# Graph attention on one core: q at the edges for two quads beside the next pair's first layers, in two PSUM banks shared with the transposes

## The chip, the core and the metric

The kernel runs on one core of a Trainium2 chip. A core has five engines that run their own instruction streams: TensorE (PE; PEld is its weight load), VectorE (DVE), ScalarE (ACT), GpSimd (POOL) and SyncE (SP). [...] The metric is the device time of one execution in microseconds. Before the change three runs took 2072.03, 2080.5 and 2083.07 us; the median is 2080.5.

## The reference

There are 6250 nodes with 128 features and 206,250 edges, sorted by receiver. Each edge has two sets of 32 features and a cutoff. Per edge a weight vector is made by two small networks, q comes from the receiver, k and v from the sender; eight heads of 16 features give eight scores, the scores scale v, the messages are summed per receiver, and the result is added to x and normalised.

```python
w_ij = silu(edge_feats @ rad_W1 + rad_b1) @ rad_W2 + rad_b2
w_ij = w_ij + (silu(chi_scalar @ sph_W1 + sph_b1) @ sph_W2 + sph_b2)
q_i = (node_feats @ Wq).reshape(-1, 8, 16)[receivers]
k_j = (node_feats @ Wk).reshape(-1, 8, 16)[senders]
alpha = (q_i * w_ij * k_j).sum(axis=-1) / sqrt(16) * cutoffs[:, None]
v_j = (node_feats @ Wv)[senders].reshape(-1, 8, 16)
out = segment_sum(alpha[..., None] * v_j, receivers, num_segments=6250) / 16
return layernorm(x + out.reshape(-1, 128))
```

## The kernel before

**Tiles.** 128 edges are a tile, four tiles a quad (512 edges), four quads a group. There are 403 quads in 101 groups (the last has three). As the edges are sorted by receiver, the receivers of a quad lie within 32 consecutive nodes and those of a group within 128, and the kernel works with one-hot matrices relative to the first of them. (If a check of this fails at run time, a general path at the end of the kernel runs instead; with these inputs it doesn't.)

**Nodes stage.** First k and v of all nodes are computed and stored in a table in DRAM (`kv_tab`). Meanwhile VectorE makes tables of the quads' and groups' first nodes (`tables`, L257).

**Edge loop.** The loop at L519 goes over groups `g` and over four slots, which take the group's quads in the order 0, 2, 1, 3; two neighbouring slots are a pair. All engines' instruction order is the order in which the program writes them; there is no scheduler. In the slot of quad `q`, TensorE does in this order:

- `weigh` (L382): two matmuls of the activated first layers with the second layers' weights, into a bank `ph` (four such banks). ScalarE adds the bias and writes `w` (L388).
- `turn_back` (L401): four transposes of the quad before, so that edges are in partitions, into the bank `pu`.
- `take_q` (L391): q at the edges, a product of the quad's 32 q rows with a one-hot over 512 edges, into the bank `pq`.
- in slots 0 and 2 `hidden` (L364): the first layers of the next pair, four matmuls on 32 rows each into `ph` banks, and four Silu on ScalarE (L378).
- in slot 1 `sum_group` (L450), which puts the part sums of an older group in their places, and `turn_q` (L338), a transpose of the next group's x rows; in slot 3 `make_q` (L345), its product with Wq.
- `sum_quads` (L426): message sums of the group before.

Float32 matmuls are two instructions each in the profile; transposes are one.

VectorE does in a slot `scores` of the quad before (L410 multiplies the transposed bank with the gathered k, L412 sums by head, L413 scales), `multiply` (L399, u = pq times w), and `messages` (L421). One-hots (L355, L360), placements (L442, L443) and statistics (L470 on) follow in some slots.

**Gathers.** GpSimd gathers k and v of the senders by indirect DMA, one per tile (L114, four per quad), 14 quads ahead into a ring of 16 buffers. Each gather waits for a mark, an instruction of TensorE in the slot that issues it, so that gathers don't run further ahead.

**SP's queue.** All plain loads and stores of the loop go through SP in program order: in slot 0 `load_q` for the next group (four register loads and four DMAs of 32 rows of x, L163), `load_xw` (128 rows of x for the layer norm, L462), `load_rel` (four DMAs that each repeat one quad's 512 relative receivers over 32 partitions, L155); in slot 1 `load_feats` (512 KB, two groups ahead, L145). Every fourth group `statistics` (L464) also stores four tiles of out (L486).

Of the kernel before, what the change touches and what calls it, by code (L numbers as in the profile page):

```python
# [2 lines left out]

# [9 lines left out]
F32 = mybir.dt.float32  # L13
BF16 = mybir.dt.bfloat16
I32 = mybir.dt.int32
AF = mybir.ActivationFunctionType
# [7 lines left out]
P = 128  # L24
# [28 lines left out]
def gnn_kernel(ctx, tc, x, src, dst, weight, edges, rad_W1, rad_b1, rad_W2, rad_b2,  # L53
# [37 lines left out]
    rel = const.tile([P, NT], F32, name="rel")  # L91
    qb_i = const.tile([1, NG * NQ], I32, name="qb_i")
    gb_i = const.tile([1, NG], I32, name="gb_i")
    rowq = const.tile([P, NG], F32, name="rowq")
    rowp = const.tile([P, NG], F32, name="rowp")
# [35 lines left out]
    feats_of, relb_of, act_of, kv_of, hot_of, hotT_of, xq_of, q_of, msg_of = ({} for _ in range(9))  # L131
    po_of, part_of, to_of, tot_of, xw_of, y0_of, u_of = ({} for _ in range(7))

# [13 lines left out]
    def quads_in(g):  # L147
        return min(NQ, QUADS - g * NQ)

    def load_rel(g):  # L150

        relb_of[g] = gp.tile([P, EQ], BF16, name="relb")
        for j in range(NQ):
            t = g * GT + j * QT
            nc.sync.dma_start(relb_of[g][j * W:(j + 1) * W, :],  # L155
                              rel_lin[t:t + QT, :].rearrange("t e -> (t e)").partition_broadcast(W))

    def load_q(g):

        xq_of[g] = gp.tile([P, D], F32, name="xq")  # L160
        for j in range(quads_in(g)):
            r = start_of(qb_i, g * NQ + j, N - W)
            nc.sync.dma_start(xq_of[g][j * W:(j + 1) * W, :], x[ds(r, W), :])  # L163

# [17 lines left out]
    with tc.tile_pool(name="nodes", bufs=1) as nodes, \  # L182
            tc.tile_pool(name="nodes_ps", bufs=2, space=PSUM) as nps:
        chunks = [(c, min(QT, NB - c)) for c in range(0, NB, QT)]
        quads_x = order[:XQ]
        xs_of, xT_of = {}, {}
        smalls = []
# [5 lines left out]

        def load_x(k):
# [62 lines left out]
        def tables():  # L257
            nc.vector.tensor_scalar(gb, qb[:, :, 0], float(N - P), None, op0=OP.min)
            nc.vector.tensor_copy(qb_i, qb[:1].rearrange("p g j -> p (g j)"))
            nc.vector.tensor_copy(gb_i, gb[:1])  # L260
            load_q(0)
            for j in range(NQ):
                b = slice(j * W, (j + 1) * W)
                nc.vector.tensor_scalar(roww[b, :], row[b, :], float(j * W), None, op0=OP.subtract)
                nc.vector.tensor_tensor(rowq[b], qb[b, :, j], gb[b], op=OP.subtract)
            nc.vector.tensor_scalar(rowq, rowq, roww, None, op0=OP.add)
            nc.vector.tensor_copy(rowwp, roww)
            nc.vector.tensor_copy(colp, col)
# [34 lines left out]
        for k in range(8):  # L303
            load_x(k)
            if k == 5:
                nc.sync.dma_start(dst_i, dst)
# [3 lines left out]
        for i, (k, n) in enumerate(work):  # L310
# [9 lines left out]
            if k + 8 < len(chunks):  # L320
                load_x(k + 8)
            if k == 4:
# [13 lines left out]

    with tc.tile_pool(name="ps", bufs=1, space=PSUM) as pp:
        def turn_q(g):  # L338
            n = quads_in(g) * W
            pt = pp.tile([P, EQ], F32, name="ph", bufs=4)  # L340
            nc.tensor.transpose(pt[:, :n], xq_of[g][:n, :], ident[:n, :n])  # L341
            xq_of[g] = gp.tile([P, P], F32, name="xqT")
            nc.scalar.activation(xq_of[g][:, :n], pt[:, :n], AF.Copy)

        def make_q(g):  # L345

            n = quads_in(g) * W
            pt = pp.tile([P, EQ], F32, name="ph", bufs=4)
            nc.tensor.matmul(pt[:n, :D], xq_of[g][:, :n], wq, start=True, stop=True)  # L349
            q_of[g] = gp.tile([P, D], F32, name="q")  # L350
            nc.scalar.activation(q_of[g][:n, :], pt[:n, :D], AF.Copy)  # L351

        def one_hots_T(g):
# [9 lines left out]

        def hidden(pair):  # L364

            for q in pair:
                g, j = divmod(q, NQ)
                r0, c0 = 2 * R * (j // 2), EQ * (j % 2)
                for i in range(2):
                    ph = pp.tile([P, EQ], F32, name="ph", bufs=4)  # L370
                    r = slice(r0 + i * R, r0 + (i + 1) * R)
                    o = nc.tensor.matmul(ph, w1[r, :], feats_of[g][r, c0:c0 + EQ],  # L372
                                         start=True, stop=True)
                    act_of[q, i] = ph
            for q in pair:
                for i in range(2):
                    act = ep.tile([P, EQ], F32, name="act", bufs=8)
                    nc.scalar.activation(act, act_of[q, i], AF.Silu, bias=b1[:, i:i + 1])  # L378
                    act_of[q, i] = act
            return o  # L380

# [8 lines left out]

        def take_q(q):  # L391
            g, j = divmod(q, NQ)
            b = slice(j * W, (j + 1) * W)
            pq = pp.tile([P, EQ], F32, name="pq")
            return pq, nc.tensor.matmul(pq, q_of[g][b, :], hotT_of[g][b, :], start=True, stop=True)  # L395

        def multiply(q, pq, w):
            u_of[q] = ep.tile([P, EQ], F32, name="u")
            nc.vector.tensor_tensor(u_of[q], pq, w, op=OP.mult)  # L399

        def turn_back(q):  # L401

            pu = pp.tile([P, QT, D], F32, name="pu")
            for t in range(QT):
                o = nc.tensor.transpose(pu[:, t, :], u_of[q][:, t * P:(t + 1) * P], ident)  # L405
            return pu, o
# [51 lines left out]

        def load_xw(g):
            r = start_of(gb_i, g, N - P)  # L460
            xw_of[g] = gp.tile([P, D], F32, name="xw")
            nc.sync.dma_start(xw_of[g], x[ds(r, P), :])  # L462

        def statistics(g):  # L464
# [4 lines left out]
            k = g - first + 1  # L469
            nc.vector.tensor_tensor(y0[:, k - 1, :], tot_of[g], xw_of[g], op=OP.add)  # L470
            st = gp.tile([P, 6], F32, name="st")
# [31 lines left out]
        def verdict():  # L503
# [5 lines left out]
            nc.vector.tensor_scalar(general, found, 0.0, None, op0=OP.is_gt)  # L509

        turn_q(0)
        make_q(0)
# [3 lines left out]
        load_rel(1)  # L516
        hidden(pairs[0])
        before = None
        for g in range(NG):  # L519
            last = g == NG - 1  # L520
            for slot, j in enumerate((0, 2, 1, 3)):
                q = g * NQ + j
                i = g * NQ + slot
                if q >= QUADS:
                    continue
                if slot == 0 and 2 <= g:
# [12 lines left out]
                if slot == 1 and 2 <= g:  # L539
                    sum_group(g - 2)  # L540
                if slot == 1 and g + 1 < NG:
                    turn_q(g + 1)
                if slot == 3:
                    make_q(g + 1)
                if 1 <= g:
                    for t in ((), (0, 1), (2, 3))[slot] if last else ((), (0, 1), (2,), (3,))[slot]:
                        marks[3] = sum_quads(g - 1, t)
# [4 lines left out]
                multiply(q, pq, w)  # L552
                if before is not None:
                    messages(before, alpha)
                before = q
                if slot == 0:
                    if g + 1 < NG:
                        load_q(g + 1)
                    if 1 <= g:
                        load_xw(g - 1)  # L560
                        if g + 1 < NG:
                            load_rel(g + 1)
                if slot == 1:
# [4 lines left out]
                    if last:  # L568
                        place(g)
                        load_xw(g)  # L570
                if slot == 2 and g + 1 < NG:
# [178 lines left out]
```

## Time and profile before

One execution was profiled. It took 2093.36 us, with a span of 2091.3 us from its first to its last instruction.

| what | value |
|---|---|
| median of the runs | 2080.5 us |
| profiled execution / its span | 2093.36 us / 2091.3 us |
| mean granted TensorE clock | 0.967 |
| TensorE busy | 1919.3 us (92%) |
| VectorE busy | 1411.4 us (67%) |
| ScalarE busy | 1000.9 us (48%) |
| GpSimd busy | 1526.5 us (73%) |
| DMA engines busy, mean in the loop | about 0.5 |

How to read the lines: a group's line in the profile gives source line, engine, operation, what it writes and reads, shapes and count, then busy time in all and the mean of one in ns, then the engine's idle time just before such instructions with what ended it. A waits line says who waited for whom: microseconds in all, number of waits, longest. A timeline line gives start and duration in us, engine, line and operation; several instructions of one kind are merged (x4). In a line of a single source line's instructions stand shortest, median and longest duration in ns, and the first and last start. A windows line gives start and end, its length, busy time and count of PE, PEld, DVE, ACT and POOL, then the granted TensorE clock, the DMA engines' share and GB/s.

### The profile page before, as it was taken

To read this page: it belongs to the slowest core of one execution; us is meant where nothing else is said; L and a number is where in the kernel's file an instruction comes from. 1 tells how busy PE (TensorE), PEld (TensorE's weight loads), DVE (VectorE), ACT (ScalarE), POOL (GpSimd) and SP (SyncE) were. 2 spreads that over 40 slices of the span, in tenths; PEclk is the share of its full clock that TensorE was granted. 3 is DMA by queue.
4 is the path that set the end of the run, shared out by engine and by line. 5 is a ranking of instruction groups with operands and counts; after the bars stand their busy time and mean duration, and the time that the engine had idled before them with its cause. 6 is when DMAs were issued, how large, how long until landed. Compare 5 with 4: busy or idle time off the path is not lost.

```text
span 2091.3 us, 33176 instructions
## 1 busy us (share of the span) xinstructions
PE 1919.3 (92%) x9843; PEld 920.2 (44%) x9843; DVE 1411.4 (67%) x2874; ACT 1000.9 (48%) x1826; POOL 1526.5 (73%) x1620
## 2 busy tenths in 40 slices
PE   8998999989999989988998989899989999899897
PEld 7444444444444434444444444444444444444443
DVE  6676766767766766766766767667667667667666
ACT  2444545544544445444445445445445444454453
POOL 6777777777777777777777777777777777777750
PEclk9999999999999999999999999999999999999998
DMA  8545455454454454445544554554554544544540
GB/s 300 156 151 153 139 154 154 138 155 145 147 157 145 146 148 151 150 146 149 153 144 143 152 152 139 155 155 139 153 149 143 157 144 146 157 144 147 149 123 14
DMA packets 166853, 310.49 MB, mean 148 GB/s; under 512 B 46530, under 2 KB 99212, under 8 KB 166668
## 3 DMA queue, kind: packets, MB, share of 16 engines
q0 software_dynamic: 76864, 209.29, 34.3%
q1 hardware_dynamic: 88316, 98.64, 14.5%
q8 instruction: 79, 1.29, 0.2%
q14 instruction: 106, 0.87, 0.1%
q10 hardware_dynamic: 1488, 0.40, 0.1%
HBM read 294.70 MB, written 13.46 MB: 147 GB/s over the span
## 4 chain that ended last, share of the span: by engine, by line
PE 76%; ACT 9%; DMA 5%; issue 3%; SPq 3%; DVE 2%; POOL 1%; ACTq 0%; DVEq 0%
PE ph L386 32%; PE pq L395 14%; PE ph L372 11%; PE pu L405 8%; PE po L431 6%; ACT act L378 6%; DMA out<-y 2%; DMA xq<-in_x 2%; PE ph L453 2%; PE ph L349 2%; POOL msg L114 1%; SPq L163 1%; ACT y L483 1%; SPq L119 1%; PE ph L341 1%
## 5 line engine op out<-in xcount | busy, mean ns | idle before, releaser
L114 POOL DMA_INDIRECT kv<-kv_tab,src_i x1580 | 1494.8, 946 | 486.2 <-issue 261.4
L386 PE MATMUL ph<-act,w 128*128 128x512 f32 x1612 | 837.0, 644 | 78.6 <-ACT act L378 78.6
L410 DVE TENSOR_TENSOR m<-pu,kv 128x512 f32<-128x512 f32 x403 | 278.6, 691 | 557.6 <-PE pu L405 554.4
L378 ACT ACTIVATE act<-ph,b 128x512 f32<-128x512 f32 x806 | 498.5, 686 | 252.8 <-PE ph L372 239.9
L388 ACT ACTIVATE w<-ph,bsum 128x512 f32<-128x512 f32 x403 | 276.5, 686 | 456.9 <-PE ph L386 455.3
L386 PEld LDWEIGHTS ph<-act,w 128*128 128x128 f32 x1612 | 285.1, 197 | 432.4 <-issue 248.1
L395 PE MATMUL pq<-hotT,q 32*128 32x512 f32 x806 | 452.8, 641 | 0.0
L372 PE MATMUL ph<-feats,w 32*128 32x512 f32 x1612 | 398.5, 629 | 0.0
L405 PEld LDWEIGHTS pu<-ident,u 128*128 128x128 f32 x1612 | 204.1, 144 | 242.2 <-issue 155.6
L399 DVE TENSOR_TENSOR u<-pq,w 128x512 f32<-128x512 f32 x403 | 274.6, 681 | 23.7 <-ACT w L388 14.3
L412 DVE TENSOR_REDUCE side<-m 128x32 f32<-128x512 f32 x403 | 280.1, 695 | 13.7
L421 DVE TENSOR_TENSOR msg<-kv,side 128x512 f32<-128x512 f32 x403 | 272.8, 677 | 0.0
L405 PE MATMUL pu<-ident,u 128*128 128x128 f32 x1612 | 247.4, 277 | 12.7 <-DVE u L399 12.7
L372 PEld LDWEIGHTS ph<-feats,w 32*128 32x128 f32 x1612 | 158.2, 185 | 73.1 <-issue 56.1
L431 PE MATMUL po<-msg,hot 128*32 128x128 f32 x3224 | 161.4, 295 | 2.9 <-ACT part L448 2.9
L395 PEld LDWEIGHTS pq<-hotT,q 32*128 32x128 f32 x806 | 118.6, 184 | 69.7 <-issue 69.7
L431 PEld LDWEIGHTS po<-msg,hot 128*32 128x32 f32 x3224 | 75.8, 113 | 108.8 <-issue 91.3
L457 ACT ACTIVATE tot<-ph 128x128 f32<-128x128 f32 x101 | 28.0, 277 | 148.2 <-PE ph L455 139.8
L413 DVE TENSOR_TENSOR side<-side,scale 128x32 f32<-128x32 f32 x403 | 80.4, 200 | 13.8
L341 PE MATMUL ph<-ident,xq 128*128 128x128 f32 (+1 forms) x101 | 30.1, 298 | 60.8 <-DMA xq<-in_x 60.4
L351 ACT ACTIVATE q<-ph 128x128 f32<-128x128 f32 (+1 forms) x101 | 27.5, 272 | 93.1 <-PE ph L349 88.2
L360 DVE TENSOR_TENSOR hot<-rel,side 128x512 f32<-128x512 f32 x101 | 68.7, 681 | 0.0
(83 smaller groups left out, 837.2 us busy)
## 6 DMA issues: line engine op xcount, KB each, us to landing
feats<-in_edges SPq DMA_DIRECT2D x101, 512.0 KB
kv<-kv_tab,src_i POOLq DMA_INDIRECT x1580
relb<-rel_lin SPq DMA_DIRECT2D x404, 32.0 KB
xw<-in_x SPq DMA_DIRECT2D x101, 64.0 KB
out<-y SPq DMA_DIRECT2D x101, 64.0 KB
xq<-in_x SPq DMA_DIRECT2D x403, 16.0 KB
kv_tab<-kv SPq DMA_DIRECT2D x12, 512.0 KB
act<-in_x SPq DMA_DIRECT2D x12, 256.0 KB
```

The costliest lines, as they stand in the source:

```text
L114: return nc.gpsimd.indirect_dma_start(out=o, out_offset=None, in_=table, in_offset=bass.IndirectOffsetOnAxis(ap=index, axis=0))
L372: o = nc.tensor.matmul(ph, w1[r, :], feats_of[g][r, c0:c0 + EQ], start=True, stop=True)
L378: nc.scalar.activation(act, act_of[q, i], AF.Silu, bias=b1[:, i:i + 1])
L386: o = nc.tensor.matmul(pw, w2[:, i, :], act_of[q, i], start=(i == 0), stop=(i == 1))
L388: nc.scalar.activation(w, pw, AF.Identity, bias=bsum)
L395: return pq, nc.tensor.matmul(pq, q_of[g][b, :], hotT_of[g][b, :], start=True, stop=True)
L399: nc.vector.tensor_tensor(u_of[q], pq, w, op=OP.mult)
L405: o = nc.tensor.transpose(pu[:, t, :], u_of[q][:, t * P:(t + 1) * P], ident)
L410: nc.vector.tensor_tensor(m, pu, kv_of[q][:, :, :D], op=OP.mult)
L412: nc.vector.tensor_reduce(alpha, m.rearrange("p t (h e) -> p t h e", e=HD), AX.X, OP.add)
L421: nc.vector.tensor_tensor(msg_of[q].rearrange("p t (h e) -> p t h e", e=HD), kv_of[q][:, :, D:].rearrange("p t (h e) -> p t h e", e=HD), a ...
L431: o = nc.tensor.matmul(po_of[g][j * W:(j + 1) * W, :], hot_of[g][:, j * QT + t, :], msg_of[g * NQ + j][:, t, :], start=(t == 0), stop=(t = ...
```

## The change

1. q at the edges is made for both quads of a pair in the even slot. A new function `q_and_hidden` takes the place of `take_q` and `hidden`: it writes alternately one q product of the pair and one first layer of the next pair, those whose rows lie on the row groups that the two q products don't use, and then the other two first layers. The odd slots have no q product.
2. The banks `pu` and `pq` become one name, `pq`, with two buffers; the transposes and the q products take them in turn.
3. In a slot the transposes of the quad before now come ahead of `weigh`. The gathers' marks are the last four of a list of the slot's TensorE instructions.
4. The x rows of a group (128 of them) are loaded once, two groups ahead, into six buffers, and serve both q and the layer norm. `load_q` and `load_xw` are gone. q's nodes are picked from these rows by a matmul with a one-hot matrix (`pick`, made by one VectorE comparison with a new table `off`), in place of a transpose of rows loaded per quad.
5. `load_rel` is one DMA instead of four.

```diff
     def load_rel(g):
         relb_of[g] = gp.tile([P, EQ], BF16, name="relb")
-        for j in range(NQ):
-            t = g * GT + j * QT
-            nc.sync.dma_start(relb_of[g][j * W:(j + 1) * W, :],
-                              rel_lin[t:t + QT, :].rearrange("t e -> (t e)").partition_broadcast(W))
-
-    def load_q(g):
-        xq_of[g] = gp.tile([P, D], F32, name="xq")
-        for j in range(quads_in(g)):
-            r = start_of(qb_i, g * NQ + j, N - W)
-            nc.sync.dma_start(xq_of[g][j * W:(j + 1) * W, :], x[ds(r, W), :])
+        r = rel_lin[g * GT:(g + 1) * GT, :].rearrange("(j t) e -> j (t e)", j=NQ)
+        nc.sync.dma_start(relb_of[g], r[:, None, :].to_broadcast([NQ, W, EQ]))
+
+    def load_x(g):
+        r = start_of(gb_i, g, N - P)
+        x_of[g] = gp.tile([P, D], F32, name="x", bufs=6)
+        nc.sync.dma_start(x_of[g], x[ds(r, P), :])
...
+            nc.vector.tensor_tensor(off, gb[:, :, None].to_broadcast([P, NG, NQ]), qb, op=OP.subtract)
+            nc.vector.tensor_scalar(off, off, row, None, op0=OP.add)
...
+        def pick(g):
+            n = quads_in(g)
+            pick_of[g] = gp.tile([P, NQ, W], F32, name="pick")
+            nc.vector.tensor_tensor(
+                pick_of[g][:, :n, :], colp[:, None, :W].to_broadcast([P, n, W]),
+                off[:, g, :n, None].to_broadcast([P, n, W]), op=OP.is_equal)
+
         def turn_q(g):
-            nc.tensor.transpose(pt[:, :n], xq_of[g][:n, :], ident[:n, :n])
+            o = nc.tensor.matmul(pt[:, :n * W], x_of[g], pick_of[g][:, :n, :], start=True, stop=True)
...
+        def hidden_of(q, i):
+            g, j = divmod(q, NQ)
+            r0, c0 = 2 * R * (j // 2) + i * R, EQ * (j % 2)
+            act_of[q, i] = pp.tile([P, EQ], F32, name="ph", bufs=4)
+            return nc.tensor.matmul(act_of[q, i], w1[r0:r0 + R, :],
+                                    feats_of[g][r0:r0 + R, c0:c0 + EQ], start=True, stop=True)
+
+        def q_at_edges(q):
+            g, j = divmod(q, NQ)
+            b = slice(j * W, (j + 1) * W)
+            pq_of[q] = pp.tile([P, EQ], F32, name="pq", bufs=2)
+            return nc.tensor.matmul(pq_of[q], q_of[g][b, :], hotT_of[g][b, :], start=True, stop=True)
+
+        def q_and_hidden(pair, following):
+            beside = 1 - pair[0] % NQ % 2 if pair else 0
+            marks, order = [], []
+            for q, n in zip_longest(pair, following):
+                if q is not None:
+                    marks.append(q_at_edges(q))
+                if n is not None:
+                    order.append((n, beside))
+                    marks.append(hidden_of(n, beside))
+            for n in following:
+                order.append((n, 1 - beside))
+                marks.append(hidden_of(n, 1 - beside))
+            for n, i in order:
+                act = ep.tile([P, EQ], F32, name="act", bufs=8)
+                nc.scalar.activation(act, act_of[n, i], AF.Silu, bias=b1[:, i:i + 1])
+                act_of[n, i] = act
+            return marks
...
-            pu = pp.tile([P, QT, D], F32, name="pu")
+            pu = pp.tile([P, EQ], F32, name="pq", bufs=2).rearrange("p (t d) -> p t d", d=D)
...
+                if before is not None:
+                    pu, mark = turn_back(before)
+                    marks.append(mark)
                 w, mark = weigh(q)
-                marks = [mark] * QT
-                if before is not None:
-                    pu, marks[1] = turn_back(before)
-                pq, marks[2] = take_q(q)
+                marks.append(mark)
                 if slot % 2 == 0:
                     u = 2 * g + slot // 2 + 1
-                    if u < len(pairs):
-                        marks[3] = hidden(pairs[u])
+                    marks.append(q_and_hidden(pairs[u - 1], pairs[u] if u < len(pairs) else [])[-1])
...
                 if i + AHEAD < len(order):
-                    gathers(order[i + AHEAD], marks)
+                    gathers(order[i + AHEAD], ([marks[0]] * QT + marks)[-QT:])
...
                 if slot == 0:
+                    if g + 2 < NG:
+                        load_x(g + 2)
                     if g + 1 < NG:
-                        load_q(g + 1)
-                    if 1 <= g:
-                        load_xw(g - 1)
-                        if g + 1 < NG:
+                        pick(g + 1)
+                        if 1 <= g:
                             load_rel(g + 1)
```

More of the change, by code (lines that the diff above doesn't have):

```diff
@@ L2 @@
 from contextlib import ExitStack
+from itertools import zip_longest
 import numpy as np
@@ L91, in gnn_kernel @@
     rel = const.tile([P, NT], F32, name="rel")
-    qb_i = const.tile([1, NG * NQ], I32, name="qb_i")
     gb_i = const.tile([1, NG], I32, name="gb_i")
+    off = const.tile([P, NG, NQ], F32, name="off")
     rowq = const.tile([P, NG], F32, name="rowq")
@@ L130, in gnn_kernel @@
             pairs[-1].append(q)
-    feats_of, relb_of, act_of, kv_of, hot_of, hotT_of, xq_of, q_of, msg_of = ({} for _ in range(9))
-    po_of, part_of, to_of, tot_of, xw_of, y0_of, u_of = ({} for _ in range(7))
+    feats_of, relb_of, act_of, kv_of, hot_of, hotT_of, x_of, q_of, msg_of = ({} for _ in range(9))
+    po_of, part_of, to_of, tot_of, xT_of, y0_of, u_of, pick_of, pq_of = ({} for _ in range(9))
     def gathers(q, marks=()):
@@ L185, in gnn_kernel @@
         quads_x = order[:XQ]
-        xs_of, xT_of = {}, {}
+        xs_of = {}
         smalls = []
@@ L191, in gnn_kernel, with load_nodes @@
             smalls.append((w1[i * R:(i + 1) * R, :], w))
-        def load_x(k):
+        def load_nodes(k):
             c, n = chunks[k]
@@ L258, in tables @@
             nc.vector.tensor_scalar(gb, qb[:, :, 0], float(N - P), None, op0=OP.min)
-            nc.vector.tensor_copy(qb_i, qb[:1].rearrange("p g j -> p (g j)"))
             nc.vector.tensor_copy(gb_i, gb[:1])
-            load_q(0)
+            load_x(0)
             for j in range(NQ):
@@ L303, in gnn_kernel @@
         for k in range(8):
-            load_x(k)
+            load_nodes(k)
             if k == 5:
@@ L320, in gnn_kernel @@
             if k + 8 < len(chunks):
-                load_x(k + 8)
+                load_nodes(k + 8)
             if k == 4:
@@ L337, in gnn_kernel @@
     with tc.tile_pool(name="ps", bufs=1, space=PSUM) as pp:
+        def pick(g):
[4 more added lines that the diff above has]
+                off[:, g, :n, None].to_broadcast([P, n, W]), op=OP.is_equal)
         def turn_q(g):
-            n = quads_in(g) * W
+            n = quads_in(g)
             pt = pp.tile([P, EQ], F32, name="ph", bufs=4)
-            nc.tensor.transpose(pt[:, :n], xq_of[g][:n, :], ident[:n, :n])
-            xq_of[g] = gp.tile([P, P], F32, name="xqT")
-            nc.scalar.activation(xq_of[g][:, :n], pt[:, :n], AF.Copy)
+            o = nc.tensor.matmul(pt[:, :n * W], x_of[g], pick_of[g][:, :n, :], start=True, stop=True)
+            xT_of[g] = gp.tile([P, P], F32, name="xT")
+            nc.scalar.activation(xT_of[g][:, :n * W], pt[:, :n * W], AF.Copy)
+            return o
         def make_q(g):
@@ L348, in make_q @@
             pt = pp.tile([P, EQ], F32, name="ph", bufs=4)
-            nc.tensor.matmul(pt[:n, :D], xq_of[g][:, :n], wq, start=True, stop=True)
+            o = nc.tensor.matmul(pt[:n, :D], xT_of[g][:, :n], wq, start=True, stop=True)
             q_of[g] = gp.tile([P, D], F32, name="q")
             nc.scalar.activation(q_of[g][:n, :], pt[:n, :D], AF.Copy)
+            return o
         def one_hots_T(g):
@@ L362, in one_hots @@
                 colp[:, None, :W].to_broadcast([P, GT, W]), op=OP.is_equal)
[L364 to L380, printed above, removed]
+        def hidden_of(q, i):
[26 more added lines that the diff above has]
+            return marks
         def weigh(q):
@@ L389, in weigh, with multiply @@
             return w, o
[L391 to L397, printed above, removed]
+        def multiply(q, w):
             u_of[q] = ep.tile([P, EQ], F32, name="u")
-            nc.vector.tensor_tensor(u_of[q], pq, w, op=OP.mult)
+            nc.vector.tensor_tensor(u_of[q], pq_of[q], w, op=OP.mult)
         def turn_back(q):
-            pu = pp.tile([P, QT, D], F32, name="pu")
+            pu = pp.tile([P, EQ], F32, name="pq", bufs=2).rearrange("p (t d) -> p t d", d=D)
             for t in range(QT):
@@ L457, in sum_group @@
             nc.scalar.activation(tot_of[g], ph[:, :D], AF.Copy)
[L459 to L462, printed above, removed]
         def statistics(g):
@@ L469, in statistics @@
             k = g - first + 1
-            nc.vector.tensor_tensor(y0[:, k - 1, :], tot_of[g], xw_of[g], op=OP.add)
+            nc.vector.tensor_tensor(y0[:, k - 1, :], tot_of[g], x_of[g], op=OP.add)
             st = gp.tile([P, 6], F32, name="st")
@@ L509, in verdict @@
             nc.vector.tensor_scalar(general, found, 0.0, None, op0=OP.is_gt)
+        pick(0)
         turn_q(0)
@@ L516, in gnn_kernel @@
         load_rel(1)
-        hidden(pairs[0])
+        load_x(1)
+        q_and_hidden([], pairs[0])
         before = None
@@ L525, in gnn_kernel @@
                     continue
+                marks = []
                 if slot == 0 and 2 <= g:
@@ L541, in gnn_kernel @@
                 if slot == 1 and g + 1 < NG:
-                    turn_q(g + 1)
+                    marks.append(turn_q(g + 1))
                 if slot == 3:
-                    make_q(g + 1)
+                    marks.append(make_q(g + 1))
                 if 1 <= g:
                     for t in ((), (0, 1), (2, 3))[slot] if last else ((), (0, 1), (2,), (3,))[slot]:
-                        marks[3] = sum_quads(g - 1, t)
+                        marks.append(sum_quads(g - 1, t))
                 if i + AHEAD < len(order):
-                    gathers(order[i + AHEAD], marks)
+                    gathers(order[i + AHEAD], ([marks[0]] * QT + marks)[-QT:])
                 if before is not None:
                     alpha = scores(before, pu)
-                multiply(q, pq, w)
+                multiply(q, w)
                 if before is not None:
@@ L569, in gnn_kernel @@
                         place(g)
-                        load_xw(g)
                 if slot == 2 and g + 1 < NG:
```

## The prediction

> **What bounds the kernel now.** I read the page's engine rows first, then the gathers' own row, the waits, and the order of time.
>
> ```profile
> span 2091.3 us, 33176 instructions
> PE 1919.3 (92%) x9843; PEld 920.2 (44%) x9843; DVE 1411.4 (67%) x2874; ACT 1000.9 (48%) x1826; POOL 1526.5 (73%) x1620
> POOL 6777777777777777777777777777777777777750
> L114 POOL DMA_INDIRECT kv<-kv_tab,src_i x1580 | 1494.8, 946 | 486.2 <-issue 261.4
> ```
> ```profile
> L114 POOL DMA_INDIRECT kv<-kv_tab,src_i x1580: 940/946/1503, 48.3 to 2023.2; - x198
> ```
> ```profile
> its engine sat idle before it (us, times) until:
>   PE pu L405: 554.4, 349
>   DMA kv<-kv_tab,src_i: 2.2, 5
> ```
> ```profile
> PE ph L341 <- DMA xq<-in_x: 60.4, 23, 4.1
> ```
>
> TensorE (PE) is 92% busy and looks like the bound. POOL at 73% looks free, but its slices are flat, and the gathers' row gives the reason: 1580 gathers start between 48.3 and 2023.2, so one every 1974.9/1579 = 1.251 us. A gather is busy 0.946 us and has 0.30 us before it; the longest wait in the loop is 0.31. So POOL issues without pause, 16 gathers or 20.01 us a group, whatever TensorE does. This is a second bound.
>
> TensorE's pace is almost the same. The product u (L399, 403 of them, first at 68.6, last at 2072.2) comes every 4.98 us, 19.94 us a group. It follows the gathers by about ten quads: m (L410) of the last quad starts at 2074.98, the last gather ended at 2024.15, and the same distance taken at every fiftieth quad is 50 to 58 us. The third fence is from L410's own row: VectorE waited for gathered rows 2.2 us in all, and for transposes 554.4. So both resources need 20 us a group, and after the last gather there are 67 us in which TensorE works off what had been gathered long before.
>
> A plain group is quicker than 19.94. Its last slot in order of time:
>
> ```profile
> 1014.49 1.98 PE L386 MATMUL ph<-act,w 128*128 128x512 f32 x4
> 1016.31 0.60 PE L405 MATMUL pu<-ident,u 128*128 128x128 f32 x4
> 1016.51 0.69 ACT L388 ACTIVATE w<-ph,bsum 128x512 f32<-128x512 f32 x1 [0.43 <-PE ph L386]
> 1016.84 1.12 PE L395 MATMUL pq<-hotT,q 32*128 32x512 f32 x2
> 1017.89 0.49 PE L349 MATMUL ph<-wq,xqT 128*128 128x128 f32 x2
> 1018.31 0.42 PE L431 MATMUL po<-msg,hot 128*32 128x128 f32 x8
> 1018.51 0.68 DVE L399 TENSOR_TENSOR u<-pq,w 128x512 f32<-128x512 f32 x1
> 1018.66 1.98 PE L386 MATMUL ph<-act,w 128*128 128x512 f32 x4
> ```
>
> From one L386 block to the next: 4.17 us, of which weights 1.82, transposes 0.53, q at the edges 1.05, q's product 0.42, sums 0.35. The L386 blocks of that group start at 1000.04, 1005.14, 1009.87, 1014.49 and 1018.66: slots of 5.10, 4.73, 4.62, 4.17, together 18.62. The other 1.3 us a group are the 23 waits of L341 for q's rows (60.4 us), the slow blocks after them, and the layer norm in every fourth group (19.7 us).
>
> **The change, part by part.** *q for two quads at once.* The odd slots lose their q product: 1.05 us twice a group, 2.1. The even slot must take the second one:
>
> ```profile
> 1002.39 0.69 PE L395 MATMUL pq<-hotT,q 32*128 32x512 f32 x1
> 1002.40 1.09 PE L372 MATMUL ph<-feats,w 32*128 32x512 f32 x3
> 1002.92 0.59 PE L395 MATMUL pq<-hotT,q 32*128 32x512 f32 x1
> 1002.93 1.43 PE L372 MATMUL ph<-feats,w 32*128 32x512 f32 x5
> ```
>
> Here products on 32 rows run side by side on four row groups: ten passes, each 0.43 us apart on one group, in about 1.82 us, because the group that holds q has four passes (4 x 0.43) and the other three have two. Now q and q' have 0.43 x 2 on two groups, one first layer each on the other two, and the remaining two first layers follow on the groups of q: again four passes at most, 1.82 us. [...] The row decides: three first layers start 0.01 us after q's first pass and ahead of its second. I take 0 for the sixth product.
>
> *Order in a slot.* Transposes now lead, then the weights. Slot 0 also loses its 0.78 us wait for a PSUM bank (PE L386 behind ACT L378: 78.6 us in 101 waits): the first hidden result now comes from a free row group after two passes instead of behind q, 0.86 us earlier, and 0.53 us of transposes stand in front of the reader. Work of the slots: 5.10 - 0.78 = 4.32; 4.73 - 1.05 + 0.2 = 3.88; 4.62; 4.17 - 1.05 = 3.12; sum 15.9. But a loop is closed more tightly: transposes 0.53, weights 1.98 to their end, w 0.04 + 0.69, u 0.05 + 0.68, then the next transposes 0.06 later: 4.03 us, the least an odd slot can take. So 4.32 + 4.03 + 4.62 + 4.03 = 17.0. In a layer norm group ScalarE's table loads and normalising (2 x 1.28 + 4 x 0.48 + 0.3, some 4.8 us) stand ahead of w; today this costs 1.1, without the slack I put 2.5, so 0.6 a group. **TensorE's own pace: 17.6 us.**
>
> *Two shared PSUM banks.* The second q product overwrites the bank that m (L410) reads. TensorE comes to it 0.53 + 1.82 = 2.35 us into the slot; m ends at about 0.64 + 0.69 = 1.33, or near 1.9 where one-hots or placements (0.68) delay VectorE. Cost 0, with some 0.4 us in hand; without that cover the four first layers behind it on TensorE wait too, and then the four activations.
>
> *Picking q's nodes.* Per group VectorE gets one 128x128 compare (0.345 us, as L442), 35 us in all on 1411; TensorE's transpose becomes a two-pass product (+0.2 us, counted). The x rows are asked for a group earlier and serve the layer norm too. On SP's queue four register loads with four 16 KB loads, one 64 KB load, and four relb loads become one, one and one. In today's trace q's rows are issued at 1005.39 to 1008.16 for a transpose at 1009.09; behind four stores of out (7.87 us in SP's rows at 253.37) they come late, and TensorE stands for up to 4.1 us. With a group of lead this goes: 60.4 us of waits, and the half-clock block after each (L386 at 267.53 took 3.78 instead of 1.98). What follows in SP's queue, relb and feats, is issued earlier as well.
>
> [...]
>
> *Gathers.* Same 1612, same table. Their wait on TensorE's marks is for a slot 14 quads back, never the last to end. I leave 1.251 us.
>
> **Sum.** TensorE gains 20.0 - 17.6 = 2.4 us a group on POOL. Its lag of some 51 us is gone after 21 of 101 groups; from then on VectorE and TensorE wait for gathered rows, and the rest of the gain has nowhere to go. The end is then the gathers' end plus a short chain. Last gather issued 2024.15; its last packets ended at 2025.7 in the trace. From today's tail: m to the end of msg 2.37 (2074.98 to 2077.35); layer norm of the group before, ahead of the last part sum on ScalarE, 2.3; from that part sum to the end of the span 8.6 (2082.71 to 2091.3). 2025.7 + 0.1 + 2.4 + 2.3 + 8.6 = 2039. Before the loop SP saves some 3.5 us of issuing ahead of the last table stores, VectorE gets 0.75 us more of tables; the first gather waits for data at 309 GB/s in those 50 us, so between -3 and +1; I take -1: span 2038, and 2 us around it, 2040 for the profiled execution (2093.4 before).
>
> The median of the runs is 2080.5, 12.9 below that execution. If the difference lies in TensorE's stalls, it vanishes when POOL is the bound (2040); if profiling slows POOL alike, it stays (2027). I take 4 of it: **2036 us**, 2.1% faster.
>
> **The rivals.** *(b) TensorE keeps some of its lag.* If its pace is between 19.5 and 20 us, 101 groups don't win 50 us: 2045 to 2080. For it: 15.9 of work and a 4.03 loop with little slack. Against it: 2 us of room. *(c) Slower: the shared bank.* The second q product waits for m, and m stands behind the last slot's VectorE work and gathered rows. It decides once m ends 2.4/2 = 1.2 us past the 0.4 in hand, in both even slots; at 2 us past it a group would take 17.6 + 3.2 = 20.8, and the time 2080 + 101 x 0.8 = 2160. For it: m would wait for gathers all the time in the forecast. Against it: a pair needs m 0.7, q and first layers 1.9, transposes 0.5, weights 2.0, w 0.7, u 0.7, transposes 0.5, weights 1.8 = 8.8 us from one such wait to the next, and the gathers give it 10. *(d) The gather pace falls* below 1.251, and the end with it: under 2018. Nothing in its 940 to 1503 ns row points to it.
>
> [...] Here the clock fell at the 4 us waits, and the plain stretch of 0.78 us waits ran at full clock:
>
> ```profile
> 262.00:269.00 7.00, 4.16 (x25) 2.14 (x24) 2.93 (x7) 0.55 (x2) 5.17 (x7) 0.73 0.59 159
> 282.40:300.00 17.60, 16.82 (x91) 8.09 (x92) 12.49 (x26) 8.70 (x16) 13.28 (x15) 1.00 0.49 152
> ```
>
> Forecast waits are about 1 us a slot, so I take the row: no loss. [...]
>
> **How the numbers follow.** Forecast 0.80 (own range 2022 to 2050), b 0.10 (half of it past 2070), c 0.07, d 0.03. Under 0.5% (10 us) the runs cannot be told from no change: faster 0.80 + 0.03 + 0.05 = 0.88, same 0.05, slower 0.07. Range 2018 to 2060, which leaves out d, c and the upper part of b.
>
> **What would show it.** Right: gathers still 1.25 us apart with the last near 2022; VectorE's m waiting for gathered rows by hundreds of us; L341's successor without DMA waits; less than 20 us from the last gather to the end. Wrong: m still waiting for transposes and a tail of 50 us (b), TensorE's q rows waiting for m (c), a lower granted clock, or gaps over 0.31 us between gathers.

## The result, and the profile after

The changed kernel takes 2045.1 us, the median of four runs (2043.11 to 2047.67), against 2079.16 us for the kernel before in the same session: a ratio of 0.984, with a 95% interval of 0.981 to 0.987. It is 1.6% faster. The forecast was 2036 us with a range of 2018 to 2060; the time lies inside, 9 us above the forecast. The profiled execution took 2046.02 us. In two of the five sessions behind this text the kernel before took 2514 and 2522 us instead of about 2080, so each ratio below is against the kernel before of the same session.

The engine rows of the page:

```profile
span 2044.3 us, 31162 instructions
PE 1752.4 (86%) x9944; PEld 877.5 (43%) x9944; DVE 1449.0 (71%) x2976; ACT 967.3 (47%) x1826; POOL 1527.3 (75%) x1620
```

The source line of the gathers (shortest, median and longest in ns, then first and last start):

```profile
L115 POOL DMA_INDIRECT kv<-kv_tab,src_i x1580: 942/946/1581, 47.9 to 2023.5; - x198
```

The source line of m, and what VectorE waited for ahead of it:

```profile
L429 DVE TENSOR_TENSOR m<-pq,kv x403: 681/692/694, 67.3 to 2027.2; 128x512 f32<-128x512 f32 x135
its engine sat idle before it (us, times) until:
  DMA kv<-kv_tab,src_i: 179.6, 126
```

TensorE lost 167 us of busy time, POOL nothing. The gathers come as before: (2023.5 - 47.9)/1579 = 1.251 us apart, and the last one starts within 0.3 us of where it started before. What changed is the work behind them. The last m starts 3.6 us after the last gather instead of 52; VectorE waits for gathered rows 179.6 us instead of 2.2. The distance from the end of a quad's last gather to its m falls along the loop: 46.7 us at quad 10, 35.8 at 30, 23.8 at 50, 12.4 at 70, 3.3 at 110, and then 1.8 to 7.4 us until the end. It is under 4 us for the first time at quad 97, so the lag is gone after some 24 groups; from there a group takes 20.0 us again.

TensorE's part of the order of time, in a plain group of the stretch where it still catches up (the six products' passes are shown for the first slot; "..." leaves other work out):

```profile
281.32 1.88 PE L411 MATMUL ph<-act,w 128*128 128x512 f32 x4
283.13 0.69 PE L385 MATMUL pq<-hotT,q 32*128 32x512 f32 x1
283.14 0.69 PE L378 MATMUL ph<-feats,w 32*128 32x512 f32 x1
283.15 0.69 PE L385 MATMUL pq<-hotT,q 32*128 32x512 f32 x1
283.15 0.69 PE L378 MATMUL ph<-feats,w 32*128 32x512 f32 x1
283.67 0.59 PE L385 MATMUL pq<-hotT,q 32*128 32x512 f32 x1
283.68 0.59 PE L378 MATMUL ph<-feats,w 32*128 32x512 f32 x1
283.68 0.59 PE L385 MATMUL pq<-hotT,q 32*128 32x512 f32 x1
283.69 1.44 PE L378 MATMUL ph<-feats,w 32*128 32x512 f32 x5
285.06 0.42 PE L450 MATMUL po<-msg,hot 128*32 128x128 f32 x8
285.41 0.66 PE L424 MATMUL pq<-ident,u 128*128 128x128 f32 x4
285.91 1.88 PE L411 MATMUL ph<-act,w 128*128 128x512 f32 x4
...
289.41 0.63 PE L424 MATMUL pq<-ident,u 128*128 128x128 f32 x4 [1.04 <-DVE u L418]
289.87 1.88 PE L411 MATMUL ph<-act,w 128*128 128x512 f32 x4
...
294.15 1.88 PE L411 MATMUL ph<-act,w 128*128 128x512 f32 x4
...
298.10 1.88 PE L411 MATMUL ph<-act,w 128*128 128x512 f32 x4
```

From one L411 block to the next: 4.59, 3.96, 4.28 and 3.95 us, together 16.78 (18.62 before). Both q products and all four first layers, twelve passes, take 283.13 to 285.06, 1.93 us. In the kernel before, ten passes took 1.91 us from their first to the next instruction (the other passes left out):

```profile
1012.22 0.69 PE L395 MATMUL pq<-hotT,q 32*128 32x512 f32 x1
...
1014.13 0.43 PE L431 MATMUL po<-msg,hot 128*32 128x128 f32 x8
```

The odd slot's TensorE waits 1.04 us for u: the loop of transposes, weights, w and u sets that slot, not the work in it.

### The profile page after: what moved, and what is told of

Read it like the earlier page. It is cut to its first block, busy times and chain, and to the rows that moved or that the text cites. A ratio compares the mean times of both kernels' runs of the same rounds, so it can differ in the third digit from the quotient of the medians.

```text
span 2044.3 us, 31162 instructions
## 1 busy us (share of the span) xinstructions
PE 1752.4 (86%) x9944; PEld 877.5 (43%) x9944; DVE 1449.0 (71%) x2976; ACT 967.3 (47%) x1826; POOL 1527.3 (75%) x1620
## 4 chain that ended last, share of the span: by engine, by line
PE 54%; DVE 17%; DMA 13%; ACT 10%; issue 6%; POOL 1%; DVEq 0%; ACTq 0%; SPq 0%; POOLq 0%
PE ph L411 25%; DMA kv<-kv_tab,src_i 12%; PE pq L385 11%; PE pq L424 9%; DVE u L418 6%; PE ph L378 5%; ACT w L413 4%; DVE m L429 4%; ACT act L403 3%; DVE side L431 2%; PE pk L222 2%; ACT y L497 2%; PE po L450 1%; DVE msg L440 1%; DVE hotT L364 1%
## 5 line engine op out<-in xcount | busy, mean ns | idle before, releaser
L411 PE MATMUL ph<-act,w 128*128 128x512 f32 x1612 | 812.6, 629 | 4.5 <-ACT act L403 4.5
L378 PE MATMUL ph<-feats,w 32*128 32x512 f32 x1612 | 474.8, 635 | 0.0
L424 PE MATMUL pq<-ident,u 128*128 128x128 f32 x1612 | 269.4, 292 | 232.4 <-DVE u L418 229.9
L429 DVE TENSOR_TENSOR m<-pq,kv 128x512 f32<-128x512 f32 x403 | 278.0, 690 | 231.7 <-DMA kv<-kv_tab,src_i 179.6
L411 PEld LDWEIGHTS ph<-act,w 128*128 128x128 f32 x1612 | 291.0, 201 | 219.5 <-issue 209.2
L424 PEld LDWEIGHTS pq<-ident,u 128*128 128x128 f32 x1612 | 175.6, 145 | 384.2 <-issue 156.0
L385 PE MATMUL pq<-hotT,q 32*128 32x512 f32 x806 | 295.1, 663 | 36.0 <-DVE m L429 35.8
L385 PEld LDWEIGHTS pq<-hotT,q 32*128 32x128 f32 x806 | 82.8, 193 | 242.5 <-issue 168.7
L450 PE MATMUL po<-msg,hot 128*32 128x128 f32 x3224 | 156.6, 287 | 2.9 <-ACT part L467 2.9
L450 PEld LDWEIGHTS po<-msg,hot 128*32 128x32 f32 x3224 | 72.9, 110 | 110.4 <-issue 83.2
L364 DVE TENSOR_TENSOR hotT<-relb,side 128x512 f32<-128x512 bf16 x101 | 68.7, 681 | 0.0
L357 PEld LDWEIGHTS ph<-wq,xT 128*128 128x128 f32 (+1 forms) x202 | 39.7, 197 | 51.9 <-issue 51.1
L472 PEld LDWEIGHTS ph<-part,to 128*128 128x128 f32 (+1 forms) x202 | 38.6, 192 | 49.6 <-issue 28.9
## 6 DMA issues: line engine op xcount, KB each, us to landing
relb<-rel_lin SPq DMA_DIRECT2D x101, 128.0 KB
```

What stands on the lines that cost most here:

```text
L378: return nc.tensor.matmul(act_of[q, i], w1[r0:r0 + R, :], feats_of[g][r0:r0 + R, c0:c0 + EQ], start=True, stop=True)
L385: return nc.tensor.matmul(pq_of[q], q_of[g][b, :], hotT_of[g][b, :], start=True, stop=True)
L411: o = nc.tensor.matmul(pw, w2[:, i, :], act_of[q, i], start=(i == 0), stop=(i == 1))
L429: nc.vector.tensor_tensor(m, pu, kv_of[q][:, :, :D], op=OP.mult)
L450: o = nc.tensor.matmul(po_of[g][j * W:(j + 1) * W, :], hot_of[g][:, j * QT + t, :], msg_of[g * NQ + j][:, t, :], start=(t == 0), stop=(t = ...
```

## The experiments

### One part alone

The change has two halves: q for two quads with shared banks and new order (parts 1 to 3), and the x rows, the picking and the single relb transfer (parts 4 and 5). Each was put into the kernel before alone. x_only:

```diff
 def turn_q(g):
-    nc.tensor.transpose(pt[:, :n], xq_of[g][:n, :], ident[:n, :n])
+    o = nc.tensor.matmul(pt[:, :n * W], x_of[g], pick_of[g][:, :n, :], start=True, stop=True)
...
-        load_q(g + 1)
+        load_x(g + 2)
+        pick(g + 1)
```

> The kernel before with parts 4 and 5 alone: x rows loaded two groups ahead, q's nodes picked from them, one relb transfer; q at the edges, the order in a slot and the banks stay. Theory (the gathers' pace is the end's floor, and any part that brings TensorE under 20 us a group for long enough gets the whole gain): without the waits for q's rows a group takes (3 x 18.6 + 19.7) / 4 = 18.9 us, the lag of 51 us is gone after some 46 groups, and the time is that of the changed kernel, 2040 to 2052 us. Rival (each part has its own share and the shares add up; both parts together gave 34 us): 18.9 against 17.8 us a group is about half of it, so 2058 to 2068. Rival (the x part does nothing, the gain is all from q): 2070 to 2083.

q_only:

```diff
-pq = pp.tile([P, EQ], F32, name="pq")
+pq_of[q] = pp.tile([P, EQ], F32, name="pq", bufs=2)
...
-marks[3] = hidden(pairs[u])
+marks.append(q_and_hidden(pairs[u - 1], pairs[u] if u < len(pairs) else [])[-1])
```

> The changed kernel with the old loads: q's rows per quad, a slot ahead, transposed as before; four relb transfers; the layer norm loads its own rows. Parts 1 to 3 stay. Theory (gathers are the floor): a plain group 16.6 us, waits for q's rows of 1 to 2 us a group in the mean still there, about 18.5; whole gain again, 2040 to 2052 us. Rival (shares add up): 2058 to 2068. Rival (the waits for q's rows were the whole gain, or come sooner as TensorE is faster, and eat it): 2070 to 2083.

Beside a kernel before of 2083.45 us, x_only took 2045.31 (ratio 0.982, 0.978 to 0.985) and q_only 2047.32 (0.983, 0.979 to 0.987). Either half gives what the whole change gives. Gathers and m's waits of x_only, then of q_only:

```profile
L114 POOL DMA_INDIRECT kv<-kv_tab,src_i x1580: 942/946/1531, 49.2 to 2024.6; - x198
```
```profile
DVE m L418 <- DMA kv<-kv_tab,src_i: 159.8, 82, 5.5
```
```profile
L115 POOL DMA_INDIRECT kv<-kv_tab,src_i x1580: 942/946/1329, 48.2 to 2023.6; - x198
```
```profile
DVE m L423 <- DMA kv<-kv_tab,src_i: 163.7, 131, 4.5
PE ph L342 <- DMA xq<-in_x: 21.7, 12, 3.7
```

In each the last gather starts within 1.4 us of the kernel before's and m waits for gathered rows by some 160 us. The distance from gather to m is first under 4 us at quad 124 in q_only and at quad 199 in x_only (97 in the kernel after): the smaller saving needs longer to work off the lag, and has the time for it. A change whose gain is capped by a second bound gives this: the first microsecond a group that is saved on TensorE counts, and the second is spent waiting. A reading in which each half has a share of 34 us that adds up falls.

### The gathers made slower

If the gathers' issue is the bound, then 97 more of them cost their full price in the kernel after, and with them both kernels end alike, as TensorE is then nowhere late. One gather a group into a spare buffer that nobody reads:

```diff
+        if marks and q % NQ == 0:
+            gather(ep.tile([P, 2 * D], F32, name="spare", bufs=4), kv_tab, src_i[:, q * QT:q * QT + 1])
```

> The changed kernel with one more gather in 97 of the groups, into a buffer that nothing reads. Theory: the last gather is 97 x 1.251 = 121 us later and the end goes with it: 2160 to 2172 us. Rival (TensorE or its waits set the end, POOL has slack): within 5 us of 2045.

> The kernel before with the same extra gather in 97 groups. Theory: with 21.3 us a group for gathers even the old TensorE order (19.9 us) is ahead, and the two kernels end alike: 2160 to 2178 us, within 1% of the changed kernel with extra gathers. Rival (the change still gives its 1.6% when gathers are slower): 2195 to 2205.

They took 2164.45 us (after) and 2166.62 us (before). The added gathers' rows, and where the others now end, of the kernel after with them:

```profile
L115 POOL DMA_INDIRECT kv<-kv_tab,src_i x1580: 940/946/1331, 47.7 to 2145.0; - x198
L115 POOL DMA_INDIRECT spare<-kv_tab,src_i x97: 942/946/951, 93.1 to 2135.0; - x97
```

and of the kernel before with them:

```profile
L114 POOL DMA_INDIRECT kv<-kv_tab,src_i x1580: 942/946/1767, 47.5 to 2145.0; - x198
```

97 gathers at 1.251 us are 121 us; the kernel after lost 119.4 (2164.45 - 2045.1, its time in the first session; x_only took 2045.31 in this one). Both kernels' last gathers start at 2145.0, and the times differ by 0.1%: with gathers this slow the change is worth nothing. The kernel before lost only 83 us by the same addition (2166.62 - 2083.45), because its TensorE lag was already there and is swallowed: its m is first within 4 us of the gathers at quad 145.

### The gathers made cheap: what TensorE's side gained

The opposite lifts the cover. Half of each quad's gathers are replaced by one plain load of 256 table rows through SP. The bytes stay the same and POOL's issuing is halved; the rows of these edges' own senders are left out, so the output is another one:

```diff
-        for t in range(QT):
+        r = (q * 512) % (NB * P - 2 * P)
+        for t in range(QT // 2):
             o = gather(kv[:, t, :], kv_tab, src_i[:, q * QT + t:q * QT + t + 1])
...
+        nc.sync.dma_start(kv[:, 2:, :], kv_tab[r:r + 2 * P, :].rearrange("(p n) d -> p n d", p=P))
```

> The kernel before, but two of the four tiles of each quad are not gathered: one plain load of fixed table rows from SP's queue fills them, so the scores and messages of those edges come from other nodes' rows. POOL's work is halved (10 us a group), the bytes moved are the same. Theory: TensorE's pace of 19.9 us a group was a bound of its own, and the time stays within 15 us of 2079. Rival (TensorE waited for gathers in a way that the trace puts elsewhere): under 2040.

> The changed kernel with the same halved gathers (other nodes' rows for two tiles of each quad). Theory: without the gathers' floor TensorE's own pace shows, 16.8 us in three groups and 20.9 in the fourth, 17.8 x 101 = 1800, with 58 us ahead of the loop and 20 behind it 1870 to 1895 us. Rival (another wait of the changed kernel, of the shared banks or of the loop over w and u, sets 20 us a group): 2030 to 2050.

> The kernel before with parts 4 and 5 alone (x rows early, pick, one relb), gathers halved as above. Theory: 18.9 us a group, 1907 + 80 = 1975 to 2000 us. If the early rows saved nothing on TensorE: 2065 to 2090.

> Parts 1 to 3 alone (q for two quads, banks, order) with the old loads, gathers halved as above. Theory: plain groups 16.6 us, and waits for q's rows that grow as the slots get shorter, 18 to 19 us a group: 1900 to 2000 us. If q at the edges saved nothing: 2065 to 2090.

| kernel | time us | pace of u, us a group | against half_before |
|---|---|---|---|
| half_before | 2144.41 | 20.02 | |
| half_x_only | 2036.36 | 18.92 | -1.10 |
| half_q_only | 1940.19 | 17.96 | -2.06 |
| half_after | 1934.18 | 17.91 | -2.11 |

Three of the four totals lie 36 to 50 us above what was expected; only half_q_only lies in its range. The kernel before took 2513.62 us beside them, and u starts at 107 to 110 us instead of 66 to 69, so some 40 us of each total are the stage ahead of the loop. The pace is therefore taken from the loop, from the first and last start of u over 402 slots, four to a group. The rows, in the table's order:

```profile
L401 DVE TENSOR_TENSOR u<-pq,w x403: 678/679/693, 106.8 to 2118.8; 128x512 f32<-128x512 f32 x135
```
```profile
L409 DVE TENSOR_TENSOR u<-pq,w x403: 678/679/693, 109.6 to 2011.2; 128x512 f32<-128x512 f32 x135
```
```profile
L414 DVE TENSOR_TENSOR u<-pq,w x403: 680/692/693, 108.2 to 1913.3; 128x512 f32<-128x512 f32 x135
```
```profile
L420 DVE TENSOR_TENSOR u<-pq,w x403: 681/691/692, 109.6 to 1909.9; 128x512 f32<-128x512 f32 x135
```

Half_before goes at 20.02, near the 19.94 of the kernel before in its own profile, and half_after's groups take 16.75, 20.87, 17.29 and 16.75 us in turn (medians), where the kernel after takes 16.77, 20.92, 17.31 and 16.77 while it catches up. So the loop itself was not disturbed in these four. With the same bytes half_after's group is 2.1 us under the 20.0 of the gathers: what held it there is POOL's issuing and not the amount of data. (That the plain loads read neighbouring rows and the gathers scattered ones is not separated.) What the change does to TensorE's side is 2.1 us a group, 212 us over 101 groups, of which 34 come out in the time. And the halves don't add here either (1.10 + 2.06 is not 2.11). With q for two quads in place, the earlier x rows bring nothing more: half_before waits 70.6 us for q's rows in 21 waits, half_q_only 3.4 us in 2. Why is argued, not shown: its layer-norm groups take 20.86 us in the median and half_after's 20.87, so TensorE comes late to the rows by itself.

### The kernel after once more, and two attempts at the end of it

If a layer norm ahead of the last part sums lengthens the end, another order shortens it. The edit, tail, closes the statistics one group earlier and writes the last part sums ahead of them:

```diff
-            if k == LB or g >= NG - 3:
+            if k == LB or g >= NG - 4:
...
-        statistics(g - 1)
         part_sums(g)
+        statistics(g - 2)
         sum_group(g)
+        statistics(g - 1)
         statistics(g)
```

A second kernel, best, also sets `XQ = 9` (8 before): for one more quad the senders' x rows are gathered before the loop and k and v computed from them, so four gathers of table rows fewer.

> The changed kernel unaltered, beside the two versions that follow. 2041 to 2048 us.

> The changed kernel with another order after the last gather: groups 96 and 97 are normalised and stored one group earlier, the last part sums are copied ahead of the layer norm of group 98, the normalising tiles have four buffers. Theory: the 20 us from the last gather to the end are a chain over ScalarE's layer norm, which stands ahead of the part sums that TensorE waits for (3 us), and VectorE's layer norm ahead of the last m (1.4 us); this saves 3 to 6 us, 2038 to 2043. Rival (the tail is TensorE's lag, or the stores of out set it): within 1 us of the changed kernel.

> The tail version with nine quads instead of eight taken from x while POOL waits for the table (its gap of 5 us ahead of the first table gather). Theory: four table gathers fewer behind the gap, 4 x 1.251 = 5.0 us less, of which the gap gives 4.6: a further 4 to 5 us, 2033 to 2039 us. Rival (the gap is not there for other work, or the nodes stage gets longer): no difference to the tail version.

All three missed. The kernel before took 2521.79 us beside them, and they took 2512.79, 2516.92 and 2524.5: ratios of 0.997 (0.995 to 0.999), 0.998 (0.996 to 1.000) and 1.001 (0.999 to 1.004). So the kernel after is worth 0.3% here instead of 1.6%. A window of its repetition (busy time of PE, PEld, DVE, ACT, POOL, then clock, DMA share, GB/s):

```profile
500.00:1500.00 1000.00, 764.99 (x4014) 367.59 (x4014) 592.52 (x1217) 401.38 (x746) 634.82 (x670) 0.89 0.41 121
```

and of the kernel after in its first session:

```profile
500.00:1500.00 1000.00, 852.43 (x4827) 415.99 (x4826) 700.81 (x1436) 474.75 (x894) 756.60 (x800) 0.95 0.48 145
```

POOL does 670 instructions in a thousand microseconds instead of 800, and the other engines do 15 to 17% less. So the gathers no longer come without pause: POOL waits for TensorE (97.6 us behind L411 alone), and 384.8 us of waits ahead of L424's weight loads have no releaser in the profile. The gathers alone are not the bound here, and the forecast does not hold for it; what the bound is stays open. The attempts at the end could not be judged there.

Best2 is best with one addition: a Sqrt on ScalarE after `part_sums(g - 1)`, so that its table (a load of 1.28 us at 2023.93 in the kernel after) is loaded before the last layer norms ask for it.

```diff
+        nc.scalar.activation(gp.tile([P, 1], F32, name="early", bufs=1), eps, AF.Sqrt)
```

> The tail and best edits together with one more: a one-column square root right after the last copy of group 99's part sums, so that ScalarE's table for it is loaded while it has nothing to do. Where the kernel before takes 2080 us (gathers every 1.251 us): nine quads from x save 4.6 us ahead of the loop; after the last gather m starts as soon as its rows are there (1.2 us less) and the chain from it to the last layer norm is 8 instead of 10.9 us. 2034 to 2039 us against 2045.1 of the changed kernel; ratio to the kernel before 0.978 to 0.981. If the table gathers' end isn't what the tail hangs on: 2043 to 2047. Where the kernel before takes 2510 us and more, the version is within 0.5% of it.

Beside a kernel before of 2077.95 us it took 2046.36 (ratio 0.986, 0.983 to 0.988): no gain over the kernel after's 2045.1, and a miss by at least 7 us. The end of the kernel after in order of time:

```profile
2027.15 1.26 ACT L497 ACTIVATE y<-y,shift,rs 128x128 f32<-128x128 f32 x3 [0.44 <-DVE shift L494]
2027.16 0.69 DVE L429 TENSOR_TENSOR m<-pq,kv 128x512 f32<-128x512 f32 x1
...
2028.32 0.25 ACT L467 ACTIVATE part<-po 128x128 f32<-128x128 f32 x1
...
2028.63 2.77 PE L450 MATMUL po<-msg,hot 128*32 128x128 f32 x16 [2.88 <-ACT part L467]
...
2038.02 0.49 ACT L497 ACTIVATE y<-y,shift,rs 128x128 f32<-128x128 f32 x1 [0.47 <-DVE shift L494]
```

Best2's gathers, its last m and its last y:

```profile
L115 POOL DMA_INDIRECT kv<-kv_tab,src_i x1576: 942/949/1368, 48.5 to 2022.9; - x197
```
```profile
2025.71 0.69 DVE L429 TENSOR_TENSOR m<-pq,kv 128x512 f32<-128x512 f32 x1 [1.70 <-DMA kv<-kv_tab,src_i]
...
2034.21 0.49 ACT L497 ACTIVATE y<-y,shift,rs 128x128 f32<-128x128 f32 x1 [0.42 <-DVE shift L494]
```

The chain did get shorter: m now waits for nothing but its rows, and the last y comes 8.5 us after it, not 10.9. But the four saved gathers, 5.0 us, are nearly eaten. The gathers start 0.6 us later and come 1.2536 us apart (1974.4/1575), 0.0024 more than in the kernel after, which over 1575 of them is 3.8 us; the median gather takes 949 ns instead of 946, and why is open. And from the end of the last y to the end of the span go 7.3 us instead of 5.8. Best2's profiled span, 2042.0 us, is 2.3 shorter, but it is that of the shortest of its six runs (2043.83 to 2050.65). What follows the last store isn't in the trace, so that part is open too.

## Why the prediction was right, and where it was off

**Two bounds.** Right, and shown from both sides: 97 more gathers cost 119 us in the kernel after, half the gathers lets it go at 17.91 us a group, and a half of the change gives all of the gain. Rival (b) is out: no lag is left. So is (d): the gathers keep 1.251 us. But the time is then no test of the 17.6 us that the prediction gave TensorE's side: x_only, forecast at 18.9, ends alike. Half_after tests it, with 17.91. The waits of m for gathered rows, forecast at hundreds of us, came to 180.

**The sixth product costs nothing.** Right. Twelve passes take 1.93 us where the step said 1.82, but ten had taken 1.91, so the sixth product added 0.02. The rows show the products side by side, as the row of the kernel before did: two q products and two first layers start within 0.02 us (283.13 to 283.15), each ahead of the second pass of the product written before it. The second passes come some 0.54 us later, with the last two first layers behind those.

**Slots.** The step gave 4.32, 4.03, 4.62, 4.03; measured 4.59, 3.96, 4.28, 3.95. The sum of 17.0 was 0.2 too high. The loop over u as the floor of the odd slots was right to 0.1 us. The weights' wait for a bank, which was to go, fell from 78.6 us to 4.5.

**The layer-norm group.** Mis-sized: 2.5 us were put on it, and it takes 4.1 more than a plain group (20.9 against 16.8). In order of time:

```profile
303.55 1.28 ACT L490 ACT_TABLE_LOAD   x1
...
305.59 1.65 ACT L497 ACTIVATE y<-y,shift,rs 128x128 f32<-128x128 f32 x4 [0.44 <-DVE shift L494]
...
307.14 0.67 ACT L413 ACTIVATE w<-ph,bsum 128x512 f32<-128x512 f32 x1
...
307.84 0.69 DVE L418 TENSOR_TENSOR u<-pq,w 128x512 f32<-128x512 f32 x1 [0.59 <-ACT w L413]
...
308.68 0.63 PE L424 MATMUL pq<-ident,u 128*128 128x128 f32 x4 [3.54 <-DVE u L418]
```

w stands on ScalarE behind the table load and four normalisations, u behind w, and the transposes that lead the next slot wait 3.5 us. The group behind takes 17.3. The misses leave (2 x 16.8 + 20.9 + 17.3)/4 = 17.9 us a group for the 17.6 of the sum, and 24 groups for the 21 until the lag is gone. None of them moved the end.

**The shared banks.** The price of 0 held for the end, though the wait exists: TensorE's q products waited for m 35.8 us in 30 waits, and their weight loads 73.2 us in 52, none of them ahead of 430 us, when the lag is nearly gone. That is rival (c)'s wait at a small fraction of its size; half_q_only, which has the same banks, keeps 17.96.

**The x rows and relb.** The waits for q's rows are gone from the list, and picking costs TensorE 0.39 us a group. No run isolates the one-transfer relb; nothing in the list waits for it. It is issued 101 times with 128.0 KB, where 404 issues of 32.0 KB were. With the fewer transfers of relb and x, packets under 512 B fell from 46530 to 34022.

**The clock.** No loss was taken, on forecast waits of about 1 us a slot. The mean fell from 0.967 to 0.952, with 40 windows at half clock (28 before). 38 of the 40 follow within 7 us on a TensorE wait of 1.0 to 3.5 us. Of the 16 waits of 3.54 us, which layer-norm groups have, 12 are followed by such a window, of the 81 waits of 1.0 to 1.5 us only 6. So waits were longer than forecast, and the row I chose did not speak for them. In the loop the loss costs no time: x_only, with a mean clock of 0.983, takes 2045.31 us all the same. (Behind the loop it may count, see the end.) The trace has windows behind long and shorter waits: 12 behind 3.54 us, others behind waits of 2.1 and 2.2 us. The window of the prediction that ran at full clock still does:

```profile
282.40:300.00 17.60, 16.20 (x102) 7.90 (x100) 14.51 (x31) 8.27 (x16) 13.33 (x15) 1.00 0.45 138
```

**The end, where the 9 us are.** The span was forecast at 2038 and is 2044.3:

| term of the sum | forecast | measured | off by |
|---|---|---|---|
| last gather's end | 2023.15 | 2024.49 | +1.3 |
| from there to the last m | 1.65 | 2.67 | +1.0 |
| from m to the end | 13.3 | 17.1 | +3.8 |

The gain of 1 us ahead of the loop did not last: the first gather starts at 47.9 instead of 48.3, but from the first start to the last it is 1975.7 us instead of 1974.9. The last m finds its rows at 2025.9 and starts at 2027.16, since VectorE has the reciprocal and shift of an older layer norm ahead of it. The step that was off most is the chain behind m. I put 2.3 us between the end of msg and the last part sum, where the old tail has 5.4 (2077.35 to 2082.71), and took the other 3 for TensorE's lag. They are there again. TensorE's sums wait for a part that ScalarE copies only behind y, and then they run at half clock, in the kernel before (granted clock 0.50 from 2075 to 2081):

```profile
2076.45 2.77 PE L431 MATMUL po<-msg,hot 128*32 128x128 f32 x16 [2.88 <-ACT part L448]
```

and in the kernel after, where L450 also waits 2.88 us and takes 2.77. Sixteen such matmuls a little earlier, and the window of the end (clock 0.52, the third number from the right):

```profile
2024.17 0.64 PE L450 MATMUL po<-msg,hot 128*32 128x128 f32 x16
```
```profile
2027.00:2034.00 7.00, 5.37 (x28) 4.15 (x28) 3.16 (x8) 1.93 (x6) 0.00 (x0) 0.52 0.10 29
```

The layer norm of the group before stands behind these sums, and the last part sum behind it, 5.4 us after msg again (2029.54 to 2034.89). How much of the 3 us is the wait and how much the clock, no run separates; in best2 the wait is gone, and eight such matmuls still take 1.84 us. The other 0.8 us of the term lie behind the last part sum. From m to the end took 16.3 us before and takes 17.1 now.

The rest is the step from profile to runs. I took 4 us of the 12.9 that the profiled execution lay above the median. After the change it lies 0.9 above. That fits a difference that was TensorE's lag, which is gone: of the seven runs of the kernel before beside x_only, 2073 to 2088 us, the two shortest have a granted clock of 0.971 and the four longest 0.968, and the four runs of the kernel after lie within 4.6 us. No run isolates it. So 6.2 from the span and 3.1 from this step, less 0.3 since the execution lies 1.7 above its span and not 2, is 9 us.

## What to carry to other kernels

When two engines need almost the same time per round, a saving on the one that looks busy is worth only the lag it has built up behind the other: here 34 of 212 us. An engine's busy share does not show that it is saturated (POOL had 75%); the spacing of its instructions does, first and last start over the count. Then ask what half of the change would give, and what the same change gives with the other bound made dearer: two cheap runs that told more than the sum.

## What the hardware showed that I had not expected

- The issue of a gather was steady to three digits, 1.251 us, in the kernels before and after, in x_only and q_only and in both runs with a spare gather, with VectorE and TensorE busy or waiting; in best2 it was 1.254.
- Two tenths of a per cent in that issue pace weighed as much in best2 as three saved gathers (3.8 us).
- In the kernel after TensorE fell to half clock for 3.4 or 6.8 us behind single waits from about 1 to 3.5 us (38 times), not only behind the longest; and 4 of the 16 longest, 3.54 us, have no such window behind them.
